# Five scalings of x moved ahead of a GpSimd product in a two-stage attention kernel

## The chip, the cores and the metric

The kernel runs on one core of a Trainium2 chip. A core has five engines that run side by side and meet only at semaphores: TensorE (PE in the profile; its weight loads are PEld), VectorE (DVE), ScalarE (ACT), GpSimd (POOL) and SyncE (SP, which issues transfers). Each takes its own instructions strictly in the order in which the program lists them. The metric is the device time of one execution in microseconds (us), as the median of several runs.

## What is computed

`x` and `ctx` are 32 sequences of 256 tokens with 256 features, all float32. Cut to what matters:

```python
# first layer: 16-head attention; only the result of batch 0 is used
tgt2 = attention(x @ Wq.T, ctx @ Wk.T, ctx @ Wv.T)[0]
f = x + tgt2                                   # for every batch

# second layer
norm_X   = layernorm(ctx, norm1_w, norm1_b)
norm_F   = layernorm(f, norm2_w, norm2_b)
attended = attention(norm_F, norm_X, norm_X, 1/16)       # "the first attention" below
h        = gelu(attended @ fc1_w.T + fc1_b)              # 256 -> 4 features
cross    = h @ fc2_w.T + fc2_b                           # 4 -> 256
norm_c   = layernorm(cross, norm3_w, norm3_b)
self_a   = attention(norm_c, norm_c, norm_c, 1/16)       # "the second attention"
out      = norm_F + gamma2 * (cross + gamma1 * self_a)
```

As `h` has four features, everything behind GELU is carried in rows of five or six numbers for each token (the four, a one, a norm), and the normalization's variance comes from a small Gram matrix. The full 256 features appear again only at the output, where `norm_F` is added. `norm_F` without its weight stands in SBUF as `x_all`; multiplying `x_all` by `norm2_w` is the scaling that this case is about.

## The kernel before

**Data.** `x_all` holds all 32 batches of x in SBUF, 128 partitions by 32 by 2 by 256. It is loaded, has the first layer's result added, and is normalized in place (`norm_x`, L333 on GpSimd and L338 on ScalarE). TensorE then transposes one batch (`turn_x`, L202 in the profile, tile pt_x), and from then on nothing of the attention reads this batch of `x_all`. (The rows stand at half their normalized size, and the weight at twice its own.) So at any time between its transpose and the addition at the output, the batch has to be multiplied by `norm2_w`: `scale_skip(n)`, one GpSimd multiplication of 128 x 512 numbers (L776, `x_all<-x_all,w_bc`). There are 32 of these.

**First stage.** A loop of 32 steps, `first_step(s)`, makes the first attention for batch `s`: scores on TensorE (L785, tile sc), their maximum on VectorE (L795, nm), the exponential on ScalarE (L798, e), the transpose of e (L202, pt_e, two steps later), and for each group of four batches the product with the values (L364, pv). Quads (groups of four batches) are numbered `q`. The tables `between` and `beside` place other work by step number: parts of what follows GELU, for pairs of quads, and the first scores of the second attention. The list `scaled_at` says in which step batch n is scaled: entry n is the step.

**GELU and what follows it, for a pair of quads k.** `hide` makes its argument (L1001 rd_f, L1007 and L1009 pre, on VectorE in this stage), `activate` is GELU on ScalarE (L1010, writes v_sl, with a table load ahead of it and one behind it). Then:

- `third_a`: w_m, GpSimd's product with the Gram matrix (L1024, 128 x 400)
- `third_b`: vg, a VectorE sum (L1038), and vgv, a GpSimd product (L1044)
- `third_c`: var, a VectorE sum (L1053); on GpSimd ve (L1060), the power r (L1062), u_sl (L1065) and w_k (L1024, 128 x 576)
- `third_d`: a VectorE sum into t_sl (L1069)

Pair 2 (quads 4 and 5) has its GELU and `third_a` in `between` of step 30, `third_b` beside step 30, `third_c` in `between` of step 31. Within a step, the scalings come before `between`:

```python
        for n, at in enumerate(scaled_at):
            if s == at:
                scale_skip(n)
        ...
        for f, *args in between:
            f(*args)
```

**Second stage.** From L1267 on the order is written out by hand as a string of words, `order`; each word issues one piece of work: `q7@s1+k6@et` products on TensorE, `max7` maxima on VectorE (L1211), `exp7` on ScalarE (L1224), `o5` and `add5` the output's product (L452) and its addition to `x_all` (L1229 on VectorE), `turn_*` transposes, `uT`, `tT`, `vT` copies out of PSUM. `pre6`, `gelu6`, `m3`, `vg3`, `vgv3`, `var3`, `r3` are the same steps as above for pair 3, with `pre6` on GpSimd, and `scale15` calls `scale_skip(15)`. Each finished pair of batches is stored by a transfer from SyncE (L1230).

Of the kernel before, what the change touches and what calls it, by code (L numbers as in the profile page):

```python
# [27 lines left out]
def tile_xattn_seq(  # L28
# [103 lines left out]
    k6 = const.tile([NK, D], F32)  # L132
# [735 lines left out]
    ]  # L868


    scaled_at = [25, 26, 26, 27, 27, 28, 29, 29, 31, 31]

    first_ends = [ends]

# [390 lines left out]


    order = """  # L1267
    turn_t2 scale10 q7@s1+q6@et t_k2 tT2 turn_n7 max7 scale11 k5@s0 n7 turn_v0 exp5
    turn_u4 pre6 vT0.v max6 uT4 scale12 o0@s1+o1@s0 gelu6 turn_t3 add0 sums1 tT3 m3
    k4@et+q9@s1 col1.v add1 scale13 turn_a1 exp4 turn_u5 max9 scale14 q8@s0 uT5 vg3  # L1270
    q11@s1+k6@et a1 vgv3 var3 turn_v1 max8 r3 exp6 sums2 vT1.v k7@s0+q10@et col2 max11
    turn_a2 exp7 turn_t4 max10 o3@s1 tT4 a2 o2@et+k9@s0 add3 scale15 turn_v2 exp9 sums3
    vT2.v t_k3 scale16 o5@s0+k8@s1 col3 add2 turn_a3 exp8 scale17 turn_u7 add5 o4@et uT7
    scale18 a3 q15@s0+q14@s1 add4 scale19 turn_t5 max14 turn_u6 tT5 turn_v3 scale20
    uT6.v vT3 k10@et+k11@s1 max15 scale21 sums4 exp11 turn_t7 exp10 scale22
    q12@s1+q13@s0 tT7.v col4.v turn_a4 max12 scale23 sums5 a4 k15@et+o6@s1 col5 scale24
    max13 turn_a5 exp15 turn_v4 scale25 add6 k14@s0 vT4 a5 scale26 o8@s1+o7@et exp14
    turn_t6 add8 scale27 sums7 tT6 add7 turn_v5 col7 scale28 o9@s1+k12@s0 vT5 k13@et
    add9 exp12 scale29 turn_a7 exp13 o10@s0+o11@s1 scale30 a7 sums6 add10 scale31
    turn_v7 col6 add11 vT7 turn_a6 o15@s0+o14@et a6 turn_v6 add15 vT6 o12@s1 add14  # L1280
    o13@s0 add12 each13
    """

    def turn_a(g):
# [101 lines left out]
```

## Time and profile before

| | |
|---|---|
| median of 3 runs | 222.96 us (222.87 to 223.15) |
| the profiled execution | 223.92 us, its span 222.1 us |
| TensorE clock granted in it | 0.992 |
| VectorE busy / ScalarE busy / GpSimd busy | 78% / 66% / 76% of the span |
| GpSimd's scalings, L776 | 32, together 39.8 us, 1.274 us each (1.262 to 1.293) |

The span is the time from the first to the last instruction of one profiled execution; the time of an execution includes what lies around it. An instruction's duration is its own; since an engine can begin the next instruction just before the last one ends, the distance from start to start of scalings in a row is a little shorter than 1.274. The chain that ended last is found by walking back from the last instruction to what released it, again and again. An engine's idle time counts only where it is on this chain, and the share of busy time is a mean over stages with different limits.

### The profile page before, as it was taken

What the parts mean: (1) busy time and instruction counts of PE and PEld (TensorE: products, weight loads), DVE (VectorE), ACT (ScalarE), POOL (GpSimd) and SP (SyncE); (2) the same over time, 40 slices, a digit from 0 to 9 for tenths busy, and PEclk for the clock granted to TensorE, in tenths of its full rate; (3) what the DMA queues carried; (4) which work ended last, traced back from release to release, by engine and by line L of the source; (5) the groups of instructions that cost most, each with busy time, mean ns of one, the idle gap of its engine ahead of it and who ended that gap; (6) DMA issues with size and microseconds to landing.
All of it is one profiled execution on the core that took longest, in us unless ns stands there. A gap on an engine that the chain in (4) does not pass through costs nothing.

```text
span 222.1 us, 4959 instructions
## 1 busy us (share of the span) xinstructions
PE 208.2 (94%) x1797; PEld 153.8 (69%) x1797; DVE 174.4 (78%) x416; ACT 146.4 (66%) x300; POOL 169.1 (76%) x268
## 2 busy tenths in 40 slices
PE   7999988899999999999999999999999999999960
PEld 6866646566778789788797797786757666655630
DVE  1687998899989789998878684596457789978791
ACT  2445787599998669667867987448694675545510
POOL 6037768776899999989929989999239979999700
PEclk9999999999999999999999999999999999999996
DMA  6689997999994999809000000000000040632786
GB/s 218 231 287 369 389 387 228 178 247 243 262 172 155 312 255 260 155 13 180 1 3 1 0 1 9 0 3 0 3 1 0 3 173 18 244 138 94 280 315 259
DMA packets 18054, 33.81 MB, mean 152 GB/s; under 512 B 1191, under 2 KB 2158, under 8 KB 18030
## 3 DMA queue, kind: packets, MB, share of 16 engines
q1 hardware_dynamic: 12990, 24.33, 30.2%
q0 software_dynamic: 3696, 7.34, 18.9%
q10 hardware_dynamic: 1344, 1.84, 2.4%
q8 instruction: 14, 0.23, 0.4%
q14 instruction: 10, 0.08, 0.1%
HBM read 17.73 MB, written 8.39 MB: 118 GB/s over the span
## 4 chain that ended last, share of the span: by engine, by line
PE 71%; DVE 17%; ACT 4%; POOL 4%; issue 2%; DVEq 0%; ACTq 0%; POOLq 0%
PE sc L785 19%; DVE st L211 5%; PE o L452 5%; PE pt_c L202 4%; PE pt_e L202 4%; PE pt_x L202 4%; PE k L452 4%; PE pu L364 4%; PE pv L364 3%; PE q L452 2%; PE sc L452 2%; PE pf L364 2%; DVE nm L795 2%; PE ph L364 2%; PE p_idle L156 2%; DVE x_all L1229 2%
## 5 line engine op out<-in xcount | busy, mean ns | idle before, releaser
L785 PE MATMUL sc<-nxT,nfT 128*128 128x256 f32 x256 | 62.4, 386 | 0.7 <-ACT nfT L767 0.7
L785 PEld LDWEIGHTS sc<-nxT,nfT 128*128 128x128 f32 x256 | 45.7, 190 | 12.1 <-issue 5.3
L798 ACT ACTIVATE e<-sc,nm 128x256 f32<-128x256 f32 x64 | 26.9, 473 | 25.0 <-DVE nm L795 24.8
L776 POOL TENSOR_TENSOR x_all<-x_all,w_bc 128x512 f32<-128x512 f32 x32 | 39.8, 1274 | 0.0
L795 DVE TENSOR_REDUCE nm<-sc 128x2 f32<-128x512 f32 x32 | 22.0, 688 | 17.7 <-PE sc L785 12.6
L767 ACT ACTIVATE nfT<-pt_x,bq,wq 128x256 f32<-128x256 f32 x64 | 33.2, 580 | 1.6 <-PE pt_x L202 1.3
L211 DVE BATCH_NORM_STATS2 st<-x_all 128x6 f32<-128x256 f32 x64 | 23.1, 409 | 0.2
L202 PE MATMUL pt_x<-ident,x_all 128*128 128x128 f32 x132 | 20.9, 280 | 1.1 <-POOL x_all L333 0.9
L202 PE MATMUL pt_c<-ident,cq 128*128 128x128 f32 x132 | 19.9, 278 | 0.9 <-ACT nfT L767 0.4
L1229 DVE TENSOR_TENSOR x_all<-o,x_all 128x1024 f32<-128x1024 f32 (+1 forms) x19 | 18.1, 993 | 2.9 <-PE o L452 2.4
L1224 ACT ACTIVATE eT<-k 128x512 f32<-128x512 f32 (+1 forms) x19 | 14.3, 799 | 9.1 <-PE k L452 7.8
L211 DVE BATCH_NORM_STATS2 st<-cq 128x6 f32<-128x256 f32 x56 | 20.1, 402 | 0.0
L202 PE MATMUL pt_e<-ident,e 128*128 128x128 f32 x128 | 19.1, 274 | 0.0
L202 PEld LDWEIGHTS pt_x<-ident,x_all 128*128 128x128 f32 x132 | 15.4, 143 | 4.5 <-POOL x_all L333 1.7
L807 ACT COPY eTq<-pt_e 128x512 f32<-128x512 f32 x31 | 17.9, 585 | 0.2 <-PE pt_e L202 0.2
L307 POOL TENSOR_SCALAR cq<-cq,rs_b,nmr_b 128x256 f32<-128x256 f32 x32 | 17.9, 574 | 0.0
L202 PEld LDWEIGHTS pt_e<-ident,e 128*128 128x128 f32 x128 | 15.6, 141 | 3.0 <-issue 0.4
L202 PEld LDWEIGHTS pt_c<-ident,cq 128*128 128x128 f32 x132 | 15.5, 143 | 2.3 <-ACT nfT L767 0.9
L352 DVE COPY nxT<-pt_c 128x512 f32<-128x512 f32 x23 | 15.5, 674 | 1.0 <-PE pt_c L202 1.0
L452 PE MATMUL o<-w_out,vt 32*128 32x256 f32 x128 | 13.3, 400 | 0.6 <-ACT vt L1102 0.5
L452 PE MATMUL k<-tt,ut 32*128 32x256 f32 x112 | 13.6, 397 | 0.0
L1211 DVE TENSOR_REDUCE t_sl<-q 128x4 f32<-128x1024 f32 (+1 forms) x12 | 12.3, 1041 | 0.3 <-PE q L452 0.2
(224 smaller groups left out, 429.5 us busy)
## 6 DMA issues: line engine op xcount, KB each, us to landing
out_dram<-x_all SPq DMA_DIRECT2D x15, 512.0 KB
x_all<-att POOLq DMA_DIRECT2D x7, 1024.0 KB, 8.5
cq<-in_ctx_dram SPq DMA_DIRECT2D x6, 1024.0 KB
x_all<-in_x_dram SPq DMA_DIRECT2D x4, 1024.0 KB
x_all<-in_x_dram SPq DMA_DIRECT2D x1, 2048.0 KB
x_all<-in_x_dram SPq DMA_DIRECT2D x1, 1792.0 KB
cq<-in_ctx_dram ACTq DMA_DIRECT2D x1, 1024.0 KB
cq<-in_ctx_dram SPq DMA_DIRECT2D x1, 768.0 KB
```

The source lines that it names most:

```text
L202: nc.tensor.transpose(pt[:, dc, t * P : (t + 1) * P], src[:, t, dc * P : (dc + 1) * P], ident)
L211: nc.vector.bn_stats(st[:, t, :], src[:, t, :])
L307: nc.gpsimd.tensor_scalar(row, row, rs[:, i + t, :], nmr[:, i + t, :], ALU.mult, ALU.add)
L364: nc.tensor.matmul(pg[SL * b : SL * (b + 1), 0, :], weights(kc, b), moving[:, b, kc, :], start=(kc == 0), stop=(kc == NC - 1),)
L452: nc.tensor.matmul(dst[i][:, t, :], lhs[r : r + SL, t * P : (t + 1) * P], rhs[r : r + SL, :], start=True, stop=True,)
L767: nc.scalar.activation(nfT_of[n][:, dc, :], px[:, dc, :], AF.Identity, bias=bq[:, dc : dc + 1], scale=wq2[:, dc : dc + 1],)
L776: nc.gpsimd.tensor_mul(x_all[:, n], x_all[:, n], w2_bc.unsqueeze(1).to_broadcast([P, NC, D]))
L785: nc.tensor.matmul(sc[:, qt, :], nfT[:, dc, qt * P : (qt + 1) * P], nxT[:, dc, :], start=(dc == 0), stop=(dc == NC - 1),)
L795: nc.vector.tensor_reduce(nm, sc, AX.X, ALU.max, negate=True)
L798: nc.scalar.activation(e[:, qt, :], sc[:, qt, :], AF.Exp, bias=nm[:, qt : qt + 1])
L807: copy(eT_of[q][:, b], turned(e_of.pop(n), "et", f"e_{n}"))
L1229: nc.vector.tensor_add(xs, po, xs)
```

## The change

Batches 10 to 14 are scaled earlier. The list `scaled_at` has 15 entries where it had 10, and the words `scale10` to `scale14` leave the hand-written order, so that this keeps 17 scalings, 15 to 31:

```diff
-    scaled_at = [25, 26, 26, 27, 27, 28, 29, 29, 31, 31]
+    scaled_at = [25, 26, 26, 27, 27, 28, 29, 29, 29, 29, 30, 30, 30, 31, 31]
...
-    turn_t2 scale10 q7@s1+q6@et t_k2 tT2 turn_n7 max7 scale11 k5@s0 n7 turn_v0 exp5
-    turn_u4 pre6 vT0.v max6 uT4 scale12 o0@s1+o1@s0 gelu6 turn_t3 add0 sums1 tT3 m3
-    k4@et+q9@s1 col1.v add1 scale13 turn_a1 exp4 turn_u5 max9 scale14 q8@s0 uT5 vg3
-    q11@s1+k6@et a1 vgv3 var3 turn_v1 max8 r3 exp6 sums2 vT1.v k7@s0+q10@et col2 max11
+    turn_t2 q7@s1+q6@et t_k2 tT2 turn_n7 max7 k5@s0 n7 turn_v0 exp5 turn_u4 pre6 vT0.v
+    max6 uT4 o0@s1+o1@s0 gelu6 turn_t3 add0 sums1 tT3 m3 k4@et+q9@s1 col1.v add1 turn_a1
+    exp4 turn_u5 max9 q8@s0 uT5 vg3 q11@s1+k6@et a1 vgv3 var3 turn_v1 max8 r3 exp6 sums2
+    vT1.v k7@s0+q10@et col2 max11
```

The rest of the order is the same words with other line breaks; source lines behind it move up by one. By the list, step 29 now scales batches 6 to 9 (before: 6 and 7), step 30 scales 10, 11 and 12 (before: none) and step 31 scales 13 and 14 (before: 8 and 9). On GpSimd this makes three scalings in a row ahead of pair 2's w_m into eight; two stay between vgv and ve; and the two ahead of pre, the one between pre and pair 3's w_m and the two between that w_m and its vgv are gone. No instruction of another engine changes its place.

More of the change, by code (lines that the diff above doesn't have):

```diff
@@ L1267, in tile_xattn_seq @@
     order = """
-    turn_t2 scale10 q7@s1+q6@et t_k2 tT2 turn_n7 max7 scale11 k5@s0 n7 turn_v0 exp5
-    turn_u4 pre6 vT0.v max6 uT4 scale12 o0@s1+o1@s0 gelu6 turn_t3 add0 sums1 tT3 m3
-    k4@et+q9@s1 col1.v add1 scale13 turn_a1 exp4 turn_u5 max9 scale14 q8@s0 uT5 vg3
-    q11@s1+k6@et a1 vgv3 var3 turn_v1 max8 r3 exp6 sums2 vT1.v k7@s0+q10@et col2 max11
[L1272 to L1281, printed above, removed]
+    turn_t2 q7@s1+q6@et t_k2 tT2 turn_n7 max7 k5@s0 n7 turn_v0 exp5 turn_u4 pre6 vT0.v
+    max6 uT4 o0@s1+o1@s0 gelu6 turn_t3 add0 sums1 tT3 m3 k4@et+q9@s1 col1.v add1 turn_a1
+    exp4 turn_u5 max9 q8@s0 uT5 vg3 q11@s1+k6@et a1 vgv3 var3 turn_v1 max8 r3 exp6 sums2
+    vT1.v k7@s0+q10@et col2 max11 turn_a2 exp7 turn_t4 max10 o3@s1 tT4 a2 o2@et+k9@s0
+    add3 scale15 turn_v2 exp9 sums3 vT2.v t_k3 scale16 o5@s0+k8@s1 col3 add2 turn_a3
+    exp8 scale17 turn_u7 add5 o4@et uT7 scale18 a3 q15@s0+q14@s1 add4 scale19 turn_t5
+    max14 turn_u6 tT5 turn_v3 scale20 uT6.v vT3 k10@et+k11@s1 max15 scale21 sums4 exp11
+    turn_t7 exp10 scale22 q12@s1+q13@s0 tT7.v col4.v turn_a4 max12 scale23 sums5 a4
+    k15@et+o6@s1 col5 scale24 max13 turn_a5 exp15 turn_v4 scale25 add6 k14@s0 vT4 a5
+    scale26 o8@s1+o7@et exp14 turn_t6 add8 scale27 sums7 tT6 add7 turn_v5 col7 scale28
+    o9@s1+k12@s0 vT5 k13@et add9 exp12 scale29 turn_a7 exp13 o10@s0+o11@s1 scale30 a7
+    sums6 add10 scale31 turn_v7 col6 add11 vT7 turn_a6 o15@s0+o14@et a6 turn_v6 add15
+    vT6 o12@s1 add14 o13@s0 add12 each13
     """
```

## The prediction

> **What bounds the kernel now.** First the page's busy times and its chain of waits: who works most, and who ends last.
>
> ```profile
> PE 208.2 (94%) x1797; PEld 153.8 (69%) x1797; DVE 174.4 (78%) x416; ACT 146.4 (66%) x300; POOL 169.1 (76%) x268
> ...
> PE 71%; DVE 17%; ACT 4%; POOL 4%; issue 2%; DVEq 0%; ACTq 0%; POOLq 0%
> ```
>
> TensorE (PE) is busy 94% of the span and is 71% of the chain; GpSimd (POOL), the only engine whose instructions change place, is 4% of it. So I read next GpSimd's own timeline over the stretch that the diff touches (start, duration, engine, line, operation, in brackets the idle time ahead of it and what ended it):
>
> ```profile
> 153.35 3.75 POOL L776 TENSOR_TENSOR x_all<-x_all,w_bc 128x512 f32<-128x512 f32 x3
> 164.09 1.01 POOL L1024 TENSOR_TENSOR w_m<-v_sl,gram_m 128x400 f32<-128x400 f32 x1 [6.99 <-ACT v_sl L1010]
> 165.79 0.36 POOL L1044 TENSOR_TENSOR vgv<-vg,v_sl 128x80 f32<-128x80 f32 x1 [0.68 <-DVE vg L1038]
> 166.10 2.50 POOL L776 TENSOR_TENSOR x_all<-x_all,w_bc 128x512 f32<-128x512 f32 x2
> 168.57 0.28 POOL L1060 TENSOR_SCALAR ve<-var 128x16 f32<-128x16 f32 x1
> ...
> 172.35 1.34 POOL L1024 TENSOR_TENSOR w_k<-u_sl,gram_k 128x576 f32<-128x576 f32 x1
> 173.65 2.50 POOL L776 TENSOR_TENSOR x_all<-x_all,w_bc 128x512 f32<-128x512 f32 x2
> 176.13 0.30 POOL L1007 TENSOR_TENSOR pre<-n_all,rd_f 128x64 f32<-128x64 f32 x1
> 176.51 0.29 POOL L1009 TENSOR_TENSOR pre<-pre,fc1b_all 128x64 f32<-128x64 f32 x1
> 176.76 1.27 POOL L776 TENSOR_TENSOR x_all<-x_all,w_bc 128x512 f32<-128x512 f32 x1
> 179.03 1.03 POOL L1024 TENSOR_TENSOR w_m<-v_sl,gram_m 128x400 f32<-128x400 f32 x1 [1.00 <-ACT v_sl L1010]
> 180.01 2.50 POOL L776 TENSOR_TENSOR x_all<-x_all,w_bc 128x512 f32<-128x512 f32 x2
> 182.85 0.35 POOL L1044 TENSOR_TENSOR vgv<-vg,v_sl 128x80 f32<-128x80 f32 x1 [0.34 <-DVE vg L1038]
> ```
>
> The reader is to see two things: GpSimd stands idle for 6.99 us ahead of the product w_m at 164.09, which waits for ScalarE's GELU, and the five scalings that the change takes away (two at 173.65, one at 176.76, two at 180.01) stand in front of instructions that wait for other engines. Third, the chain in order of time, where it leaves TensorE in this stretch:
>
> ```profile
> 175.84 0.38 PE pt_v L1077 x2
> 176.22 0.02 issue
> 176.24 0.44 DVE vt L1102
> 176.68 0.04 issue
> 176.72 1.36 PE o L452 x13
> ```
>
> Here, and at 160.45 for 0.59 us in ScalarE's copy eTq, others hold TensorE up; GpSimd nowhere does between 158 and 178.
>
> **The change part by part.** It takes nothing away: 32 scalings stay, with the same operands. The order of the built instructions shows that only GpSimd's stream differs, and that every other engine still waits for the same instruction of GpSimd.
>
> *Five scalings ahead of w_m (added there).* Three in a row become eight. In the row at 153.35 three take 3.75, so 1.25 each from start to start (a single one lasts 1.27). Eight end at 153.35 + 7 x 1.25 + 1.27 = 163.37. w_m starts at 164.09 when GELU lets it: 0.72 us are left. With the longest scaling of the trace, 1.293 us, the five end at 157.10 + 5 x 1.293 = 163.57, and 0.52 are left. They need no datum that is late: their rows of x were normed and turned long before, and none of the five waits for a semaphore. Cost: 0. The cover is the wait for GELU. Without it the price would be 5 x 1.25 = 6.25 us of GpSimd, and behind it in the queue stand vgv, two scalings, ve, the power r, u_sl and w_k; VectorE's vg at 165.14 waits for w_m, and behind vg stand VectorE's maxima and nm at 168.71. nm had 0.36 us of idle time ahead of it; ScalarE's e at 169.44 waits for nm and TensorE's pt_e at 170.15 for e, on the chain. So w_m may be 0.36 us late for nothing; beyond that it costs one for one.
>
> *Two scalings between vgv and ve (166.10).* Other rows of x stand there (numbers 13 and 14 in place of 8 and 9), of the same form, each with a wait for TensorE's transposes of the same rows, which ended by 89.10 + 0.63 = 89.73 (row 14's, the 15th group pt_x of the trace). 2.50 us as before, ve at 168.57 as before: 0.
>
> *Two scalings off the front of pre (173.65).* pre follows them back to back at 176.13, so it looks as if it gained. But it also reads rd_f, VectorE's reciprocal at 175.80 with 0.25 us, done at 176.05; the way from VectorE's end to GpSimd's start is 0.08 us (vg ended at 165.14 + 0.57 = 165.71, vgv began at 165.79). That gives 176.13 again. And if pre came earlier: GELU reads its result at 178.69, when ScalarE's table load (177.40, 1.28 us, ended 178.68) is over, while pre2 was done at 176.51 + 0.29 = 176.80. Gain: 0.
>
> *One scaling off the front of the second w_m (176.76).* It ended at 178.03; w_m began at 179.03 behind GELU (178.69 + 0.26 = 178.95). Gain: 0, GpSimd only idles 2.27 us in place of 1.00.
>
> *Two scalings off the front of the second vgv (180.01).* They ended at 182.51; vgv began at 182.85 behind VectorE's vg, which ended at 182.21 + 0.56 = 182.77. VectorE's vg itself stands behind a maximum that began at 181.08, no business of GpSimd's. Gain: 0. From vgv on, GpSimd's list is the same to the end, with the 17 scalings from 188.63 on.
>
> *Other engines beside the scalings.* No row of before has GpSimd scaling in 157.10 to 163.37, so I bound what its neighbours pay by the same forms beside scalings and not: ScalarE's two copies eTq took 1.07 at 150.86 (beside) and 1.07 at 160.45 (idle GpSimd); its nfT pair 1.05 at 151.81 and 1.05 at 161.39; TensorE's eight matmuls of L785 1.73 at 150.10 and 1.73 at 162.51; VectorE's maxima nm 682 to 693 ns. One pair differs:
>
> ```profile
> 156.80 0.38 DVE L1007 TENSOR_TENSOR pre<-n_all,rd_f 128x64 f32<-128x64 f32 x1
> 157.22 0.22 DVE L1009 TENSOR_TENSOR pre<-pre,fc1b_all 128x64 f32<-128x64 f32 x1
> 158.99 0.69 DVE L795 TENSOR_REDUCE nm<-sc 128x2 f32<-128x512 f32 x1 [1.55 <-PE sc L785]
> ```
>
> Two VectorE instructions of one size, the first beside a scaling, the second just behind the last one: 379 against 224 ns; at 117.07, with GpSimd in its power (little to read), the same two at twice the size took 293 and 292. After the change the second has a scaling beside it too; it may cost 0.155 us. Behind it VectorE idles 1.55 us and GELU needs it 6.3 us later (157.44 to 163.76): 0 on the path. Cover gone, 0.155.
>
> [...]
>
> In the other direction VectorE loses its neighbour for 6.27 us (2.50 + 1.27 + 2.50). Its instructions there read PSUM and have the durations that they have elsewhere (x_all 1.22 beside, 1.21 later). A gain is bounded by TensorE, which in 176.1 to 179.0 is busy 2.82 of 2.90 us and in 173.65 to 176.1 and 179.0 to 182.85 all of the time: 0.08 us.
>
> **Sum.** 0 + 0 + 0 + 0 + 0 + 0 = 0 against the profiled execution's own span of 222.1 us (its time with what lies around the span was 223.92). The median of the three timed runs, 222.96, is 0.96 under that execution; a change of 0 leaves the median: **222.96 us**. Bounds: -0.08 (TensorE's idle time above); on the other side the 0.155 of L1009, taken as if it had no cover. The three runs of before lie from 222.87 to 223.15, which sets the rest of the width.
>
> **Rivals.** Within 0.2% (0.45 us) of 222.96 I count as no change, about what a measurement of this kernel can tell apart.
>
> *Slower: the eight scalings overrun GELU.* From a GpSimd scaling of (6.99 + 0.36) / 5 = 1.47 us on, w_m is late enough to push nm, e and pt_e. The trace's only stretching by a neighbour is 0.379 / 0.224 = 1.69; at 1.25 x 1.69 = 2.11 each, five take 10.6, w_m starts at 167.7, 3.6 late, less 0.36: about +3.2, 226.2 us. For it: such a stretching exists. Against it: all 32 scalings lie between 1.262 and 1.293 us, beside the busiest VectorE too, and VectorE is busy only 1.98 of the 7.00 us in question. To lose 0.45 us a scaling would need 1.56 us.
>
> *Faster: later work was held up by the five scalings.* If VectorE, ScalarE or TensorE ran quicker without them, or pre's start counted, the stretch from 173.65 to 182.85 would shrink. The rows above allow 0.08 us where TensorE is limited: 222.88, inside no change. To be faster by 0.45 TensorE's own matmuls would have to be slowed by GpSimd; 1.73 against 1.73 says no. Were they, by 0.45 over the 6.27 us, some 7%, the time would be 222.5.
>
> *The change doesn't do what it says:* the built order has the eight in a row, so this falls away.
>
> **Chances and range.** No change 0.86; slower by overrun 0.05, by any stretching that I don't see 0.01 more; faster 0.08. The predicted time is that of no change. The range 222.6 to 223.3 takes in -0.08 and +0.155 with the scatter of 0.28 between the runs of before; what is left out on each side are the rivals.
>
> **What would show it.** In the profile after: eight scalings from about 153.35 to 163.4, w_m still near 164.1 with some 0.7 us of idle time ahead of it by ScalarE; L1009 near 0.38; pre near 176.13, now with idle time of 2.4 us ahead of it ended by VectorE's rd_f; the second w_m and vgv at 179.0 and 182.85; 17 scalings from 188.6; a span within 0.3 of 222.1. I am wrong if w_m starts past 164.45, if pre or anything behind it starts earlier by more than 0.1, or if TensorE's rows change their durations.

## The result and the profile after

| | before | after |
|---|---|---|
| median of 6 runs | 222.99 us (222.87 to 223.68) | 230.34 us (228.92 to 231.07) |
| ratio | | 1.0305, 95% interval 1.0281 to 1.0328 |
| the profiled execution | 223.92 us, span 222.1 | 230.09 us, span 228.3 |
| mean granted clock of TensorE | 0.992 | 0.976 |

The change costs 3%, where no change was forecast. GpSimd's scalings do what was forecast. Its timeline after the change (start, duration, engine, line, operation, in brackets the idle time ahead):

```profile
152.84 9.85 POOL L776 TENSOR_TENSOR x_all<-x_all,w_bc 128x512 f32<-128x512 f32 x8
168.04 1.01 POOL L1024 TENSOR_TENSOR w_m<-v_sl,gram_m 128x400 f32<-128x400 f32 x1 [5.35 <-ACT v_sl L1010]
171.76 0.36 POOL L1044 TENSOR_TENSOR vgv<-vg,v_sl 128x80 f32<-128x80 f32 x1 [2.70 <-DVE vg L1038]
172.07 2.50 POOL L776 TENSOR_TENSOR x_all<-x_all,w_bc 128x512 f32<-128x512 f32 x2
```

The eight scalings end at 162.69 and have time to spare: w_m waits 5.35 us more for ScalarE's GELU. So GpSimd is early, and GELU is late. VectorE's timeline shows why:

```profile
156.00 0.24 DVE L1001 RECIPROCAL rd_f<-n_all 128x16 f32<-128x16 f32 x1
156.27 6.50 DVE L1007 TENSOR_TENSOR pre<-n_all,rd_f 128x64 f32<-128x64 f32 x1
162.81 0.22 DVE L1009 TENSOR_TENSOR pre<-pre,fc1b_all 128x64 f32<-128x64 f32 x1
162.95 0.68 DVE L795 TENSOR_REDUCE nm<-sc 128x2 f32<-128x512 f32 x1
163.55 0.18 DVE L821 COPY g_sl<-pt_f 128x32 f32<-128x32 f32 x1
```

L1007, a product of 128 x 64 numbers that took 0.38 us before, takes 6.50. It starts while GpSimd's third scaling runs and ends at 162.77, 0.08 us behind the eighth. In VectorE's queue nm (L795) stands behind it and starts at 162.95, though its scores were ready some 4.5 us earlier: in the list of before nm had been waiting for TensorE, and started at 158.99 (this execution runs 0.53 us ahead of that one up to here). From there the delay goes on through ScalarE's e and eTq to TensorE:

```profile
159.82 0.63 PE L364 MATMUL pv<-eTq,g_sl 128*32 128x256 f32 x6
165.04 1.91 PE L364 MATMUL pv<-eTq,g_sl 128*32 128x256 f32 x10 [4.58 <-ACT eTq L807]
166.88 0.69 PE L1077 MATMUL pt_t<-ident,t_sl 128*128 128x128 f32 x2
167.36 3.04 PE L785 MATMUL sc<-nxT,nfT 128*128 128x256 f32 x8
170.34 1.15 PE L452 MATMUL sc<-ut 32*128 32x256 f32 x16
```

TensorE stands for 4.58 us within the pv matmuls. And what it does next is slow: pv, pt_t and sc take 1.91, 0.69 and 3.04 us. The granted clock by stretch (columns: stretch, its length, busy time and number of instructions of PE, PEld, DVE, ACT and POOL, then the granted clock, DMA share and GB/s):

```profile
156.00:162.80 6.80, 4.45 (x36) 3.22 (x30) 6.74 (x3) 2.07 (x4) 6.70 (x6) 1.00 0.01 2
162.80:165.00 2.20, 0.00 (x0) 0.00 (x0) 0.92 (x3) 1.33 (x4) 0.00 (x0) 0.51 0.01 4
165.00:167.00 2.00, 1.96 (x11) 0.68 (x12) 0.01 (x1) 1.98 (x4) 0.00 (x0) 0.50 0.00 0
167.00:170.40 3.40, 3.40 (x14) 2.59 (x14) 0.83 (x2) 2.24 (x3) 1.01 (x1) 0.60 0.00 0
170.40:176.00 5.60, 5.60 (x56) 4.24 (x56) 4.92 (x10) 1.60 (x5) 4.16 (x5) 1.00 0.00 0
```

The first six pv matmuls end at 159.82 + 0.63 = 160.45. The clock is still 1.00 up to 162.80, 0.51 in the rest of the wait, 0.50 and 0.60 in the five microseconds behind it, and 1.00 again. What that costs is read from the chains of the two profiles (start, time on the chain), before:

```profile
161.09 1.05 PE pv L364 x10
162.14 0.37 PE pt_t L1077 x2
162.51 1.73 PE sc L785 x8
```

and after:

```profile
165.04 1.91 PE pv L364 x10
166.95 0.62 PE pt_t L1077 x2
167.57 2.83 PE sc L785 x8
```

pv's remaining ten matmuls, pt_t and sc take 2.21 us more together. These ten matmuls started at 161.09 before and at 165.04 after, 3.95 later (the profiled execution after was 0.53 ahead at the first six, 159.82 against 160.35). 3.95 + 2.21 = 6.16, and the spans differ by 6.2. The medians differ by 7.35: the profiled execution lies 0.93 above its median before and 0.25 below it after.

### The profile page after: what moved, and what is told of

Its sections match the earlier page's. It is cut to its first block, busy times and chain, and to the rows that moved or that the text cites. A ratio compares the mean times of both kernels' runs of the same rounds, so it can differ in the third digit from the quotient of the medians.

```text
span 228.3 us, 4959 instructions
## 1 busy us (share of the span) xinstructions
PE 209.8 (92%) x1797; PEld 154.5 (68%) x1797; DVE 180.3 (79%) x416; ACT 146.4 (64%) x300; POOL 169.2 (74%) x268
## 4 chain that ended last, share of the span: by engine, by line
PE 67%; DVE 21%; ACT 4%; POOL 4%; issue 2%; DVEq 0%; ACTq 0%; POOLq 0%
PE sc L785 18%; DVE st L211 5%; PE o L452 4%; PE pt_c L202 4%; PE pt_e L202 4%; PE k L452 4%; PE pt_x L202 4%; PE pu L364 4%; PE pv L364 3%; DVE pre L1007 3%; PE q L452 2%; DVE nm L795 2%; PE ph L364 2%; PE pf L364 2%; PE p_idle L156 2%
## 5 line engine op out<-in xcount | busy, mean ns | idle before, releaser
L785 PE MATMUL sc<-nxT,nfT 128*128 128x256 f32 x256 | 63.5, 392 | 0.7 <-ACT nfT L767 0.7
L785 PEld LDWEIGHTS sc<-nxT,nfT 128*128 128x128 f32 x256 | 46.7, 194 | 12.5 <-issue 5.3
L795 DVE TENSOR_REDUCE nm<-sc 128x2 f32<-128x512 f32 x32 | 22.0, 687 | 17.5 <-PE sc L785 11.0
L364 PE MATMUL pv<-eTq,g_sl 128*32 128x256 f32 x128 | 10.0, 405 | 4.6 <-ACT eTq L807 4.6
```

The lines of the kernel that those rows point to most:

```text
L364: nc.tensor.matmul(pg[SL * b : SL * (b + 1), 0, :], weights(kc, b), moving[:, b, kc, :], start=(kc == 0), stop=(kc == NC - 1),)
L785: nc.tensor.matmul(sc[:, qt, :], nfT[:, dc, qt * P : (qt + 1) * P], nxT[:, dc, :], start=(dc == 0), stop=(dc == NC - 1),)
L795: nc.vector.tensor_reduce(nm, sc, AX.X, ALU.max, negate=True)
```

## The experiments

All compare with the kernel before on the same chip at the same time; there, its median lay between 223.22 and 223.52 us. A "hold" is an instruction of VectorE that lasts longer beside GpSimd than it does alone, with no wait ahead of it in the profile.

**One and two scalings moved.** The list `scaled_at` gets one (or two) more entries of 29 and the order loses `scale10` (and `scale11`):

```diff
-    scaled_at = [25, 26, 26, 27, 27, 28, 29, 29, 31, 31]
+    scaled_at = [25, 26, 26, 27, 27, 28, 29, 29, 29, 31, 31]
...
-    turn_t2 scale10 q7@s1+q6@et t_k2 tT2 turn_n7 max7 scale11 k5@s0 n7 turn_v0 exp5
+    turn_t2 q7@s1+q6@et t_k2 tT2 turn_n7 max7 scale11 k5@s0 n7 turn_v0 exp5
```

> The kernel before with one scaling (batch 10) moved ahead of pair 2's w_m, so four in a row. Theory 'hold': VectorE's pre (L1007), the one instruction there that reads two operands from SBUF, cannot run while GpSimd's scalings follow each other without a gap, and ends some 0.07 us behind the last one. Counted on the times of before, the run ends at 157.10 + 1.25 = 158.35, so pre lasts about 1.6 us (156.80 to 158.43), L1009 ends at 158.7 and nm still starts at 158.99: time 222.9 to 223.2, no change. Rival 'proportional contention': each scaling beside VectorE slows its neighbours by a share, pre then lasts at most 0.4 us, and the loss of 7.4 us spreads evenly, about +1.5 us for each moved scaling: 224.4.

> Two scalings (batches 10 and 11) moved, five in a row. Theory 'hold': the run ends at 159.60, pre lasts about 2.9 us, L1009 ends at 159.93 and nm starts 0.94 us later than the 158.99 of before; TensorE's wait for ScalarE's eTq grows by as much: about +0.9, 223.9 us, or up to 0.5 more if TensorE's clock falls behind the longer wait. Rival 'proportional contention': +3.0, 226.0, with pre at 0.4 us. Rival 'threshold' (something happens only with a run as long as eight): 222.96 here too.

Measured: 223.62 us, ratio 1.0004 (0.9986 to 1.0023), with one; 224.14 us, ratio 1.0033 (1.0014 to 1.0052), with two. VectorE's timeline with one:

```profile
156.81 1.62 DVE L1007 TENSOR_TENSOR pre<-n_all,rd_f 128x64 f32<-128x64 f32 x1
158.47 0.23 DVE L1009 TENSOR_TENSOR pre<-pre,fc1b_all 128x64 f32<-128x64 f32 x1
159.00 0.69 DVE L795 TENSOR_REDUCE nm<-sc 128x2 f32<-128x512 f32 x1 [0.31 <-PE sc L785]
```

and with two:

```profile
155.99 2.85 DVE L1007 TENSOR_TENSOR pre<-n_all,rd_f 128x64 f32<-128x64 f32 x1
158.88 0.22 DVE L1009 TENSOR_TENSOR pre<-pre,fc1b_all 128x64 f32<-128x64 f32 x1
159.02 0.68 DVE L795 TENSOR_REDUCE nm<-sc 128x2 f32<-128x512 f32 x1
```

pre's duration goes from 0.38 us over 1.62 and 2.85 to 6.50 with none, one, two and five scalings moved: 1.22 to 1.24 us for each, the distance from one scaling to the next. With one it ends before nm could start anyway and costs nothing; with two nm is held, TensorE waits 0.94 us for eTq, and its clock stays at 1.00. Contention in proportion, and a threshold near eight scalings, both fall.

**pre computed by GpSimd.**

```diff
-        return hidden_sum(lo, hi, hidden_rd(lo, hi), nc.vector)
+        return hidden_sum(lo, hi, hidden_rd(lo, hi), nc.gpsimd if lo == 4 else nc.vector)
```

> The changed kernel with quads 4 and 5's pre (L1007 and L1009) computed by GpSimd in place of VectorE, between the fifth and the sixth of the eight scalings. Theory 'hold': no VectorE instruction with two SBUF inputs is left in this stretch, so nothing is held: nm at its old place, w_m within 0.3 us of 164.1 (the eight scalings and two small products end at about 164.0), time 222.6 to 223.4. Rival 'eight scalings slow VectorE, ScalarE or TensorE in general': still 228 or more.

Measured: 223.30 us, ratio 1.0011 (0.9995 to 1.0026). The eight scalings are early as in the changed kernel, and the whole loss is gone. So it is not that five more scalings slow the other engines: it is VectorE's pre. (Both L1007 and L1009 went to GpSimd here, between the fifth and the sixth scaling.)

**Operands in PSUM.** The changed kernel, but VectorE's reciprocal and first product are written to a PSUM bank, so that the product and the addition of the bias behind it each read one operand from there:

```diff
+        hp = bank("tp", f"hp_{lo}")
+        rd = hp[:, 0, 0:n].unsqueeze(2)
+        pre = hp[:, 1, 0 : n * FH].rearrange("p (n h) -> p n h", h=FH)
+        nc.vector.reciprocal(rd, n_flat[:, ts, FH:NM])
+        nc.vector.tensor_mul(pre, n_flat[:, ts, 0:FH], rd.to_broadcast([P, n, FH]))
...
+        nc.vector.tensor_add(pre2, pre, fc1b_all.unsqueeze(1).to_broadcast([P, n, FH]))
```

> The changed kernel with quads 4 and 5's reciprocal and the first product written to PSUM, so that L1007's and L1009's counterparts on VectorE read one operand from PSUM and one from SBUF, beside the same eight scalings. Theory 'only two operands in SBUF are held': both last at most 0.4 us, nm is on time, 222.7 to 223.8. Rival 'every VectorE product of two tensors is held, wherever they lie': 6 us again, 229 or more.

Measured: 223.41 us, ratio 0.9999 (0.9984 to 1.0014). VectorE's timeline:

```profile
155.83 0.23 DVE L1006 TENSOR_TENSOR hp<-n_all,hp 128x64 f32<-128x64 f32 x1
156.10 0.22 DVE L1008 TENSOR_TENSOR pre<-hp,fc1b_all 128x64 f32<-128x64 f32 x1
157.95 0.69 DVE L795 TENSOR_REDUCE nm<-sc 128x2 f32<-128x512 f32 x1 [1.63 <-PE sc L785]
```

Beside the same run of eight scalings (152.35 to 162.22) the same two instructions take 0.23 and 0.22 us. The first also writes to PSUM; the second writes to SBUF, as L1009 does, and is not held either. So beside such a run pre is held with both operands in SBUF (6.50 us) and not with one in PSUM (0.23).

**Three breaks in the run, with and without a wait.** Ahead of the scalings of batches 8, 9 and 10 GpSimd multiplies one column by 1.0; in the first kernel a column of the weight row, so that each waits for the other, in the second a column that no scaling reads:

```diff
     def scale_skip(n):
+        if 8 <= n <= 10:
+            nc.gpsimd.tensor_scalar(w2_bc[:, 0:1], w2_bc[:, 0:1], 1.0, 0.0, ALU.mult, ALU.add)
```

> The changed kernel with a GpSimd instruction on one column of the weight row (times 1.0) ahead of the scalings of batches 8, 9 and 10, which depends on the scaling before and on which the next depends, so that GpSimd stands still for some 0.08 us on either side of it. Theory 'hold until a gap': pre and L1009 slip into the first gaps, at about 157.2 to 157.9 on the times of before; nm stays at 158.99; w_m is 0.4 us later at most, inside its slack: 222.8 to 223.5. Rival 'hold until GpSimd's queue is empty', whatever small gaps there are: pre lasts until the last scaling, about 164.4: 231 us or more.

> As three_gaps, but the small GpSimd instructions work on a column that no scaling reads, so that nothing waits and GpSimd never stands still. Theory 'a standstill of GpSimd lets VectorE in': pre is held to the last scaling, 6.5 us, span 227 or more. Rival 'any instruction other than a scaling lets it in': pre ends with the third scaling, at most 0.6 us, span 221 to 223.

Measured: 223.34 us, ratio 1.0002 (0.9983 to 1.0022), with waits (pre 0.39 us); 223.35 us in one run, span 221.6, without. GpSimd's timeline of the second kernel, and VectorE's:

```profile
152.85 3.72 POOL L778 TENSOR_TENSOR x_all<-x_all,w_bc 128x512 f32<-128x512 f32 x3
156.66 0.19 POOL L777 TENSOR_SCALAR neg_half<-neg_half 128x1 f32<-128x1 f32 x1
156.81 1.28 POOL L778 TENSOR_TENSOR x_all<-x_all,w_bc 128x512 f32<-128x512 f32 x1
158.06 0.20 POOL L777 TENSOR_SCALAR neg_half<-neg_half 128x1 f32<-128x1 f32 x1
158.21 1.28 POOL L778 TENSOR_TENSOR x_all<-x_all,w_bc 128x512 f32<-128x512 f32 x1
```

```profile
156.26 0.40 DVE L1009 TENSOR_TENSOR pre<-n_all,rd_f 128x64 f32<-128x64 f32 x1
156.69 0.24 DVE L1011 TENSOR_TENSOR pre<-pre,fc1b_all 128x64 f32<-128x64 f32 x1
158.45 0.69 DVE L797 TENSOR_REDUCE nm<-sc 128x2 f32<-128x512 f32 x1 [1.53 <-PE sc L787]
```

The expectation that only a standstill of GpSimd lets VectorE in was wrong: pre took 0.40 us here too. The small instruction at 158.06 starts before the scaling ahead of it has ended (156.81 + 1.28 = 158.09), so GpSimd takes it without a pause; the one at 156.66 starts 0.09 us behind its scaling (152.85 + 3.72 = 156.57), at the moment at which pre ends (156.26 + 0.40 = 156.66). By these times VectorE was let in there, and GpSimd waited for it. The change of the kind of instruction was enough, in this one run.

**GpSimd instructions with one tensor operand.** Six, and then ten, instructions x_all times 1.0 are added to the kernel before, first behind its three scalings, then between the first and the second of them (the second edit is shown):

```diff
+        if s == 29:
+            for n in range(8, 18):
+                nc.gpsimd.tensor_scalar(x_all[:, n], x_all[:, n], 1.0, 0.0, ALU.mult, ALU.add)
         for n, at in enumerate(scaled_at):
```

> The kernel before with six GpSimd instructions of one tensor operand (x_all times 1.0, 128x512 each) behind the three scalings of the run, back to back; all scalings at their places of before. Theory 'hold by GpSimd's instructions with two tensor operands': pre is free when the third scaling ends, 0.4 us as before, span 222 to 223. Rival 'hold by any GpSimd instruction that touches SBUF': pre lasts until the sixth ends, some 5 to 6.5 us more, span 227 or more.

> The kernel before with ten GpSimd instructions of one tensor operand (0.59 us each in the run one_input, 5.9 together) between the first and the second of the three scalings, so that VectorE's pre starts in their midst. Theory 'instructions with one tensor operand let VectorE in at each end': pre lasts at most 0.9 us, span 221.5 to 223. Rival 'any run without a standstill holds': pre lasts to the end of the ten and the two scalings behind them, some 6.5 us, span 227 or more.

Measured: 223.44 us with six and 223.01 us with ten, one run each. The first run was too weak for its question: pre was over before the six began; only L1009's counterpart met them and took 0.66 us. The second run's GpSimd and VectorE timelines:

```profile
152.46 1.28 POOL L776 TENSOR_TENSOR x_all<-x_all,w_bc 128x512 f32<-128x512 f32 x1
153.81 5.87 POOL L926 TENSOR_SCALAR x_all<-x_all 128x512 f32<-128x512 f32 x10
159.65 2.50 POOL L776 TENSOR_TENSOR x_all<-x_all,w_bc 128x512 f32<-128x512 f32 x2
```

```profile
155.92 0.34 DVE L1010 TENSOR_TENSOR pre<-n_all,rd_f 128x64 f32<-128x64 f32 x1
156.29 0.55 DVE L1012 TENSOR_TENSOR pre<-pre,fc1b_all 128x64 f32<-128x64 f32 x1
158.12 0.69 DVE L795 TENSOR_REDUCE nm<-sc 128x2 f32<-128x512 f32 x1 [1.28 <-PE sc L785]
```

The ten, of 0.62 us each, start every 0.58 to 0.59 us; in even steps of 0.585 from 153.81, an estimate, two of them start at 155.57 and 156.15 and so end at 156.19 and 156.77. pre ends at 156.26 and the addition behind it at 156.84, 0.07 us behind each. So these instructions, with one tensor operand, hold VectorE too, but each only to its own end; the scalings, with two, hold it to the end of the run. The two kinds differ in the operation and the length as well, and no run parts these from the number of operands.

**A copy in pre's place.** pre on GpSimd as above, and on VectorE, in its old place, a copy from SBUF to SBUF of 5 x 256 numbers that nobody reads:

```diff
+        if lo == 4:
+            nc.vector.tensor_copy(tail, bias2)
```

> The changed kernel with pre on GpSimd (as in the run before, which took 223.30) and, in pre's old place on VectorE, a copy from SBUF to SBUF of 5x256 numbers that nobody reads. If one operand in SBUF is not enough for the hold, it lasts some 0.2 to 0.5 us and the span is 221 to 223; if a copy from SBUF to SBUF is held too, it lasts until the fifth scaling ends, some 2.5 us, and nm is late by about 0.3 to 1 us.

Measured: 223.75 us in one run. VectorE's timeline:

```profile
155.53 0.24 DVE L1004 RECIPROCAL rd_f<-n_all 128x16 f32<-128x16 f32 x1
155.69 3.23 DVE L998 COPY tail<-bias 5x256 f32<-5x256 f32 x1
158.84 0.67 DVE L795 TENSOR_REDUCE nm<-sc 128x2 f32<-128x512 f32 x1
```

The copy is held as well, for 3.23 us, past the five scalings (152.34 to 158.51) and the product of pre that follows them on GpSimd without a pause (158.48 to 158.77), until 158.92. The copy alone was not timed; a product of that size, from SBUF too, takes 0.40 us in the profile after (L655). Two operands are thus not needed for the hold. The reciprocal ahead of it, from SBUF to SBUF too, took 0.24 us beside a scaling, so it isn't the place of the operands alone either.

**TensorE kept at work.** The changed kernel with 21, then 11 matmuls that nobody reads ahead of step 30's pv:

```diff
+            if name == "v6" and at == 0:
+                for _ in range(11):
+                    nc.tensor.matmul(pg[:, 1, :], ident, w2_bc, start=True, stop=True)
```

> The changed kernel with 21 matmuls of 128x256 on TensorE (their result is read by nobody) ahead of the pv matmuls of step 30, which keep TensorE at work while VectorE's pre is held. Theory 'hold, and then a low clock': of the 6.2 us that the changed kernel's span gained, 4.58 us less the 0.61 that TensorE waited there before are the hold, and 2.21 us are the matmuls after it, which ran at a granted clock of 0.5 to 0.6 (pv 1.91 against 1.05, pt_t 0.62 against 0.37, sc 2.83 against 1.73). With TensorE at work the clock stays at 1.00, and the time is some 2.2 us under the changed kernel's 230.34: 227 to 228.5, with pre still at 6.5 us. Rival 'the matmuls are slow for another reason' (memory that GpSimd or ScalarE uses): sc stays at 2.8 us, 230 or more.

> The changed kernel unchanged, to stand beside the next run on the same chip: ratio to before 1.028 to 1.033 as measured, with VectorE's pre at 6.5 us and a granted clock of 0.5 to 0.6 in TensorE's first 5 us behind the wait.

> As warm_tensor, whose 21 matmuls took 9.23 us and so outlasted the hold by 3.7 us, with 11 of them: 11 x 0.44 = 4.8 us, over at 164.5 just before ScalarE's eTq at 165.0. Theory 'hold, and then a low clock': sc behind it takes 1.9 us in place of 3.0, and the time is 1.5 to 3 us under the changed kernel's beside it. Rival 'the clock has no part in it': the same time as the changed kernel within 0.5 us.

Measured: 21 matmuls took 9.23 us and so outlasted the hold (pv then started at 168.79, in the changed kernel at 165.04), and the expected 227 to 228.5 us was missed: 232.74 us, ratio 1.0407 (1.0378 to 1.0435), though sc behind them took 1.89 us. With 11: 227.80 us, ratio 1.0198 (1.0175 to 1.0222); the changed kernel beside it: 229.68 us, ratio 1.0289 (1.0254 to 1.0324). TensorE with 11:

```profile
159.88 4.91 PE L366 MATMUL pv<-w_bc,ident 128*128 128x256 f32 x22
164.72 1.50 PE L367 MATMUL pv<-eTq,g_sl 128*32 128x256 f32 x16
166.15 0.44 PE L1080 MATMUL pt_t<-ident,t_sl 128*128 128x128 f32 x2
166.42 1.89 PE L788 MATMUL sc<-nxT,nfT 128*128 128x256 f32 x8
```

Here VectorE's pre is held for 6.48 us as before, but sc takes 1.89 us, not 3.04, and the clock is 1.00 throughout. The two medians differ by 1.88 us: so some 1.9 us or more of the changed kernel's 6.46 is the low clock (2.21 by the chains above), and the other 4.58 (227.80 less 223.22) the hold, with whatever the 11 matmuls cost themselves. (The 0.61 us of waiting before that the expectation takes off was too much: TensorE was busy 6.89 of the 7.00 us from 157.10 to 164.10, so 0.11; the rest of it is the lead of 0.53.)

No version is faster than the kernel before. With pre out of the way the five early scalings are free, as the prediction had it, and bring nothing.

## Why the prediction was wrong

**The step that failed** is "Other engines beside the scalings". It read 379 against 224 ns as a price of 0.155 us for a neighbour, to be paid once by L1009, and saw the cover in VectorE's 1.55 us of idle time. The 379 ns were a wait: in the profile before, the last scaling ended at 153.35 + 3.75 = 157.10 and pre at 156.80 + 0.38 = 157.18, the same 0.08 us behind the run's end as in the changed kernel. The term is thus not a constant but the rest of the run, some 1.24 us for each scaling that is added behind pre's start, and it falls on L1007, which was running already, not on L1009. Five make 6.1 us (6.50 less 0.38), the cover takes 1.55, and 4.6 are left; nm was 4.5 late (162.95 against 158.99 less the lead of 0.53). The two rows stood in the prediction with the right place and the right pair of engines; what was missing was to compare pre's end with the end of the neighbour's run.

**The length of the wait, and a neighbour that holds nothing.** A wait for the end of the scaling that was running alone would have been an estimated 0.3 us (in the profile after pre starts at 156.27, and the third scaling ends at about 152.84 + 2 x 1.23 + 1.28 = 156.58); pre waited for six. Nor does every instruction of GpSimd hold VectorE as long as it lasts. The profile before has its power, of two operands, over both instructions of an earlier pre, the pair that the prediction names at 117.07:

```profile
116.53 2.92 POOL L227 TENSOR_TENSOR rs_b<-ve_b,neg_half 128x16 f32<-128x16 f32 x1
```

```profile
117.07 0.29 DVE L1007 TENSOR_TENSOR pre<-n_all,rd_f 128x128 f32<-128x128 f32 x1
117.40 0.29 DVE L1009 TENSOR_TENSOR pre<-pre,fc1b_all 128x128 f32<-128x128 f32 x1
```

They were over (117.69) 1.8 us before the power was (119.45).

**The size.** A second term was absent: TensorE's clock after 4.58 us of standing (0.50 to 0.60 in the five microseconds behind it), 1.9 us by the pair of runs, 2.2 by the chains.

**The rivals.** "Slower: overrun of GELU" had the direction, at 0.05, and the wrong place: the scalings didn't stretch (1.265 to 1.296 us after) and didn't overrun. Its path (nm, e, then TensorE) was of the kind that the delay took, but at an earlier nm (158.99, not 168.71) and from pre on, not from w_m. The stretching of 1.69 that it counted with was the wait for the run's end. That every engine waits for the same instruction of GpSimd, on which the prediction rested, holds and says nothing here: the profile shows no wait ahead of pre, only its duration (6.50 us). The engines of this kernel thus do not meet only at semaphores, as the text ahead of the prediction has it.

**What was right.** Eight scalings in about 9.9 us; pre of pair 3 behind rd_f (it now idles 2.63 us ahead of it), the second w_m behind GELU (2.22) and its vgv behind vg (2.80): none of the places from which scalings were taken gained, and in the kernels in which pre isn't held the time is that of before within 0.3%.

## What to carry to other kernels

Where GpSimd gets a longer run of two-operand instructions without a break, look up every VectorE instruction that starts beside it: here one that read both operands from SBUF (6.50 us), or (in one run) copied from SBUF to SBUF (3.23 us), stood until the run was over, and with it everything behind it in VectorE's queue, whatever the semaphores say. Three small instructions of another kind within the run (ratio 1.0002 with waits), an operand in PSUM (0.9999), or the instruction moved to GpSimd (1.0011) each took the whole loss away here. A duration that is longer beside a neighbour is first to be compared with the neighbour's end: here the two agreed within 0.07 to 0.08 us with none, one, two and five scalings moved, so it was a wait, and its length (0.38, 1.62, 2.85 and 6.50 us) was the neighbour's to decide.

## What the runs showed of the hardware

- VectorE's product of two SBUF operands was held through the rest of a run of scalings, 6.5 us, and ended 0.07 to 0.08 us behind it; between two scalings it was never let in. It was let in, within 0.1 us, at the end of a scaling that a one-operand instruction followed (0.39 and 0.40 us) and at the end of a one-operand instruction (0.34 us, and 0.55 for the sum behind it). Why the end of a scaling with another behind it doesn't do is open; successive scalings overlap by some 0.03 us in the records, but so do the one-operand instructions (0.62 us each, every 0.58 to 0.59).
- GpSimd's power, two operands and 2.92 us, held neither of the two VectorE instructions beside it (0.29 us each).
- A copy from SBUF to SBUF on VectorE was held likewise (3.23 us); a reciprocal from SBUF to SBUF (0.24), and a product and a sum with one operand in PSUM (0.22 to 0.23) were not.
- GpSimd's multiplication by a constant, 128 x 512, takes 0.62 us against 1.28 for the product of two tensors of that size.
- After 4.58 us of standing TensorE's granted clock was 0.50 for two microseconds and 0.60 in the next 3.4; after 0.94 us it stayed at 1.00. In the longer wait it was still 1.00 from 162.60 to 162.80 and 0.65 from there to 163.00, so it fell some 2.4 us behind TensorE's last matmul (160.45), well within the wait.
